# A graph layer's table stage: issue order of SyncE, load order, first columns, one helper's engine and one layout

## The chip, the cores and the metric

The kernel runs on one core of one Trainium2 chip. The metric is device time in microseconds for one launch. The engines are TensorE (PE; its weight loads are PEld), VectorE (DVE), ScalarE (ACT), GpSimd (POOL) and SyncE (SP), which here only issues DMAs and waits. Each engine works through its own queue in order.

## The reference

One relational graph layer on 625 nodes of width 512, with 20,625 edges sorted by destination, four relations, and a feed-forward block. Cut to what matters:

```python
h = max(layernorm(x), 0)
xs = h[src]
total_msg = sum over r of (xs @ W_rel[r] + b_rel[r]) * where(edge_type == r, edge_weight, 0)
agg = segment_sum(total_msg, dst) / max(segment_sum(edge_weight, dst), 1)
x1  = layer_norm(h + h @ W_self + b_self + agg)          # gain and bias ln1
ffn = gelu(x1 @ W_ffn1 + b_ffn1) @ W_ffn2 + b_ffn2
out = x + layer_norm(x1 + ffn)                           # gain and bias ln2
```

## The kernel before

Nodes stand in five blocks of 128 rows, edges in 162 tiles of 128. There are two stages.

**The table stage** computes h @ W_rel[r] for all nodes and the four relations: 20 steps (`table_rows(r, i)`, r outermost, step = 5r + i). A step is four matmuls, a scaled copy into `m` on ScalarE (L362, scaled by the inverse root that GpSimd computes, L310) and a DMA of `m` into a table in DRAM, issued by SyncE (L364). In the first five steps the next block of x is transposed in the middle of a step; VectorE computes its statistics (L343) and norm (L333) ahead of that. Two buffers hold relation weights, so the weights of relations 2 and 3 (L203) can load only when those of 0 and 1 are used up.

Messages are summed in two ways. For the **outer blocks** (0 and 4), whose edges are 31 and 32 tiles, the kernel builds a matrix of edge weights, destination by table row, and multiplies it with the kept `m`. The matrix lies in DRAM (`cells`): it is filled with zeros by a DMA (L227), then one weight per edge is scattered into it by an indirect DMA that GpSimd issues, one per column of 128 edges (L518, followed by a tiny fill, L521; 63 in all), and at last it is read back by SyncE (`load_sums`, L529), which must wait for that block's scatters. VectorE prepares columns in pieces (`line_sums`, L504 to L512: equal edges near each other are found by comparing keys and their weights added, 8 columns at a time). The place of each edge's cell comes from `line_columns`: five operations on VectorE, then twelve small ones (L468 to L480) on GpSimd.

For the **inner blocks** the message rows are gathered: in **the edge stage** GpSimd issues 99 indirect DMAs that fetch 128 rows each from the table (L942), and six for first edges (L1004). ScalarE and VectorE scale and add the rows of neighbouring tiles (L951, L969), TensorE sums them by destination with one-hot matrices (L980, L997), and the norms, the feed-forward block and the stores follow block by block. Eight buffers hold gathered rows.

Also in the table stage, the **degrees** are computed: the edge weights are split in three bfloat16 parts and written by relation into `w3` (L558), one-hot matrices `oc` are made by comparison (L581), and 172 small matmuls sum them (L599); a column of ones counts the edges. From the counts, `first_edges` finds each node's first edge group, and three indirect DMAs fetch these (L621).

What sets the order: VectorE, ScalarE, TensorE and GpSimd run in the order in which the code of the table stage is written (`manual_schedule`); SyncE's order there is left to the scheduler of the framework. Constants say at which step something is written: `COLUMNS_AT` (pieces), `LINE_AT` (the second block's places), `LOAD_AT` (the first `load_sums`), `PACE` (three scatters per step), and so on. In the edge stage a planner (`Plan`) lays out the order of all engines from estimated costs; `free = {"POOL": 3.0}` is when it lets GpSimd start, `LATE` when the second block's sums are there, both counted from the table's last matmul.

Of the kernel before, what the change touches and what calls it, by code (L numbers as in the profile page):

```python
# [16 lines left out]
P = 128  # L17
# [55 lines left out]
class Plan:  # L73
# [31 lines left out]
    def times(self):  # L105
        left, order, t = list(self.ops), [], 0.0
        free, buffers, back = {"POOL": 3.0}, dict(self.buffers), []
# [33 lines left out]
def gnn_layer(ctx, tc, x, edges, edge_line, edge_groups, w_self, w_rel, w_ffn1, w_ffn2, rows_in, brel_in, bf1_in, out, n_edges):  # L141
# [96 lines left out]
    load_x(2, 3)  # L238
    clear_cells(OUTER[0])
    load_x(3, NB)  # L240
# [208 lines left out]
    def line_columns(b, n):  # L449
# [17 lines left out]
        e = nc.gpsimd  # L467
# [74 lines left out]
    def degree_columns():  # L542
# [12 lines left out]
        w3 = early.tile([P, NT, DW], BF16, name="w3")  # L555
        nc.vector.memset(w3[:, :, DW - 1:DW], 1.0)
        for r in range(R):
            nc.vector.scalar_tensor_tensor(  # L558
                w3[:, :, r:DW - 1:R].rearrange("p t k -> p k t"), typ_f.unsqueeze(1).to_broadcast([P, 3, NT]), float(r), part,
                op0=ALU.is_equal, op1=ALU.mult)  # L560
# [26 lines left out]
    def degree_sums(j0, nj, oc, w3):  # L587

        for j in range(j0, j0 + nj):
            s = ep.starts[j]  # L590
            lo, hi = max(s, 0), min(s + W, NP)
            for q in range(lo // D, (hi - 1) // D + 1):
# [6 lines left out]
                nc.tensor.matmul(pdeg[q][:DW, a - q * D:z_ - q * D], w3[:, j, :], oc[:, j - j0, a - s:z_ - s],  # L599
# [215 lines left out]
    COLUMNS_AT, LINE_AT = (0, 2, 4, 7, 10, 12, 13, 14), 5  # L815
    LOAD_AT = (2, 4)
# [6 lines left out]
    LATE = 12.0  # L823
# [3 lines left out]
    DEGREES_AT, SPREAD_AT, FIRST_AT = (2, 3), (2, 4), (3, 0)  # L827
    chunks = [(j0, min(DG, NT - j0)) for j0 in range(0, NT, DG)]
    pieces = [(b, k, min(k + PIECE, n)) for b, _, n in outer for k in range(0, n, PIECE)]
    with tc.manual_schedule(engines={PE, DVE, ACT, mybir.EngineType.Pool}):  # L830
# [6 lines left out]

        def next_norm(i):
            nonlocal stats
            if i < NB:  # L840
                pre_norm(i, stats)
            if i + 1 < NB:
                stats = x_stats(i + 1)
# [9 lines left out]
        next_norm(0)  # L853
        hots, made = [], 0
        for k, n in ((0, 1), (1, 1), (2, 2)):
            transposed(hT[0][:, k:k + n, :], z[:, 0, k * P:(k + n) * P], f"h0_{k}")
        pre_norm(1, stats)
        line_columns(OUTER[0], sizes[OUTER[0]])
        stats = x_stats(2)
        for r in range(R):  # L860
            for i in range(NB):
                def next_transposed():
                    transposed(hT[i + 1], z[:, i + 1, :], f"h{i + 1}")
                    next_norm(i + 2)

                table_rows(r, i, next_transposed if r == 0 and i + 1 < NB else None)
                step = r * NB + i
                if step in COLUMNS_AT:
                    next_columns()
                if step == LINE_AT:  # L870
                    line_columns(OUTER[1], sizes[OUTER[1]])
                    set_limits(0)
                    for b in OUTER:
                        line_check(b, sizes[b])
# [422 lines left out]
```

## Time and profile before

| | |
|---|---|
| median of three runs | 303.07 us (301.33 to 303.23) |
| the profiled execution | 301.95 us |
| its span, first to last instruction | 300.1 us |
| PE / DVE / ACT / POOL busy | 249.5 / 186.3 / 67.6 / 199.0 us |
| mean granted TensorE clock | 0.934 |

Lines of the profile begin with a start and a duration in microseconds where they come from a view in order of time; a bracket at the end gives how long the engine stood before it, and what ended that. Groups give busy time, mean nanoseconds of one, then the standing time before them. "SPq" is SyncE's queue: an entry's duration there is the time of issuing. A row of stretches gives the stretch and its length, then pairs of busy time and count for the engines asked for, then granted clock, the share of the DMA engines and GB/s.

### The profile page before, as it was taken

How to read it: one execution, taken by the hardware profiler on the slowest of the kernel's cores; microseconds unless marked ns; L12 is line 12 of the kernel's file. 1: busy time of each engine (PE TensorE's matmuls, PEld its weight loads, DVE VectorE, ACT ScalarE, POOL GpSimd, SP SyncE). 2: the span in 40 equal slices, each digit the busy share in tenths (PEclk: the TensorE clock that was granted, in tenths of full speed). 3: DMA queues.
4: the chain of work that ended last, by engine and by line, in shares of the span. 5: the costliest groups of instructions: out<-in, count | busy, mean ns of one | idle time of the engine just before them, and what ended most of it. 6: DMA issues, size and time to landing. Idle time of an engine off the chain costs nothing.

```text
span 300.1 us, 3286 instructions
## 1 busy us (share of the span) xinstructions
PE 249.5 (83%) x1031; PEld 135.0 (45%) x1031; DVE 186.3 (62%) x417; ACT 67.6 (23%) x126; POOL 199.0 (66%) x287
## 2 busy tenths in 40 slices
PE   6869999995008999207999999899999999999891
PEld 2424444472003543003444444447659486673870
DVE  2599899999400700040468855697968889884714
ACT  2212111200000120004322221234314045250330
POOL 3638898888888888427777777677777777741000
PEclk9998999999555999956999999999999999999998
DMA  7997974000099300646667666666666776761101
GB/s 204 383 382 285 340 262 172 0 3 0 11 324 399 108 0 0 166 164 206 210 209 214 207 207 200 184 206 210 208 195 205 240 216 206 234 187 31 38 2 37
DMA packets 23743, 52.93 MB, mean 176 GB/s; under 512 B 4717, under 2 KB 8813, under 8 KB 23338
## 3 DMA queue, kind: packets, MB, share of 16 engines
q0 software_dynamic: 10512, 27.59, 31.2%
q1 hardware_dynamic: 13064, 24.97, 23.8%
q8 instruction: 9, 0.15, 0.2%
q10 hardware_dynamic: 146, 0.13, 0.1%
q14 instruction: 12, 0.10, 0.1%
HBM read 43.50 MB, written 9.18 MB: 176 GB/s over the span
## 4 chain that ended last, share of the span: by engine, by line
DMA 34%; POOL 33%; issue 15%; DVE 10%; PE 5%; ACT 1%; SPq 1%; POOLq 0%; DVEq 0%; ACTq 0%
POOL cells L518 23%; DMA ms<-table,row_i 22%; DMA xs<-in_x_dram 4%; POOL ms L942 4%; DMA ms_first<-table,x_row 4%; PE pu L736 2%; DMA table<-m 2%; PE po L754 2%; DVE ea L969 2%; POOL idle L521 2%; DVE z L1009 1%; DVE z L1000 1%; DMA cells<-weight,cell 1%; ACT ea L951 1%; POOL ms_first L1004 1%
## 5 line engine op out<-in xcount | busy, mean ns | idle before, releaser
L942 POOL DMA_INDIRECT ms<-table,row_i x99 | 95.6, 966 | 39.7 <-issue 23.0
L358 PE MATMUL pt<-wr,hT 128*128 128x512 f32 x160 | 74.9, 625 | 21.2 <-DMA wr<-in_L_gnn_W_rel_dram 21.2
L518 POOL DMA_INDIRECT cells<-weight,cell x63 | 71.5, 1134 | 18.1 <-issue 13.0
L358 PEld LDWEIGHTS pt<-wr,hT 128*128 128x128 f32 x160 | 31.2, 200 | 59.2 <-issue 58.9
L997 PE MATMUL acc<-es,oh 128*128 128x512 f32 x58 | 30.7, 628 | 15.2 <-ACT es L951 15.2
L969 DVE SCALAR_TENSOR_TENSOR ea<-ms,wgt_g,ea 128x512 f32<-128x512 f32 x40 | 30.0, 751 | 17.7 <-DMA ms<-table,row_i 14.0
L736 PEld LDWEIGHTS pu<-x1T,w_sb 128*128 128x128 f32 x320 | 37.6, 192 | 6.4 <-issue 3.8
L736 PE MATMUL pu<-x1T,w_sb 128*128 128x128 f32 (+1 forms) x320 | 38.3, 276 | 1.8 <-ACT gT L740 1.1
L951 ACT ACTIVATE ea<-ms,ed 128x512 f32<-128x512 f32 x30 | 20.7, 692 | 75.7 <-DMA ms<-table,row_i 54.7
L1075 PE MATMUL acc<-m,sums_w 128*128 128x512 f32 x80 | 36.4, 596 | 0.0
L754 PE MATMUL po<-w_sb,gT 128*128 128x512 f32 (+3 forms) x96 | 36.2, 522 | 0.0
L362 ACT ACTIVATE m<-pt,rx 128x512 f32<-128x512 f32 x20 | 13.7, 687 | 79.1 <-PE pt L358 79.1
L1075 PEld LDWEIGHTS acc<-m,sums_w 128*128 128x128 f32 x80 | 15.2, 193 | 19.7 <-issue 19.7
L754 PEld LDWEIGHTS po<-w_sb,gT 128*128 128x128 f32 (+1 forms) x96 | 16.6, 189 | 15.6 <-issue 13.5
L997 PEld LDWEIGHTS acc<-es,oh 128*128 128x128 f32 x58 | 11.1, 198 | 25.4 <-ACT es L951 17.3
L1009 DVE SCALAR_TENSOR_TENSOR z<-acc,rdeg,z 64x512 f32<-64x512 f32 (+1 forms) x13 | 9.7, 746 | 15.3 <-PE acc L997 15.1
L374 PE MATMUL pz<-ws_sb,hT 128*128 128x512 f32 x40 | 17.9, 594 | 0.8 <-DVE n_out L422 0.8
L969 DVE SCALAR_TENSOR_TENSOR es<-ms,wgt_g,ea 128x512 f32<-128x512 f32 x20 | 14.8, 742 | 2.3 <-DMA ms<-table,row_i 2.0
L740 ACT ACTIVATE gT<-pu,bf 128x128 f32<-128x128 f32 (+1 forms) x40 | 13.4, 361 | 10.9 <-PE pu L736 10.9
L951 ACT ACTIVATE es<-ms,ed 128x512 f32<-128x512 f32 x9 | 6.5, 721 | 28.8 <-DMA ms<-table,row_i 28.8
L614 DVE TENSOR_SCALAR xw<-first_edges 128x3 f32<-128x3 f32 x1 | 0.2, 163 | 20.0 <-PE first_edges L611 20.0
L374 PEld LDWEIGHTS pz<-ws_sb,hT 128*128 128x128 f32 x40 | 7.5, 190 | 9.9 <-issue 9.9
(174 smaller groups left out, 246.6 us busy)
## 6 DMA issues: line engine op xcount, KB each, us to landing
table<-m SPq DMA_DIRECT2D x20, 256.0 KB, 7.1
w_sb<-in_L_gnn_W_ffn_dram SPq DMA_DIRECT2D x2, 2048.0 KB, 11.0
wr<-in_L_gnn_W_rel_dram SPq DMA_DIRECT2D x3, 1024.0 KB, 9.8
cells<-zeros SPq DMA_DIRECT2D x2, 1280.0 KB
sums_w<-cells SPq DMA_DIRECT2D x2, 1280.0 KB
ms<-table,row_i POOLq DMA_INDIRECT x99, 3.6
rows<-in_rows_dram SPq DMA_DIRECT2D x1, 1536.0 KB, 10.3
ws_sb<-in_L_gnn_W_self_dram SPq DMA_DIRECT2D x1, 1024.0 KB, 6.0
```

The costliest lines, as they stand in the source:

```text
L358: nc.tensor.matmul(p, hT[i][:, k, :], wr_sb[r][:, k, :], start=(k == 0), stop=(k == KD - 1))
L362: nc.scalar.activation(m, p, AF.Copy, scale=rx[:, i, 1:2])
L374: nc.tensor.matmul(p[0], hT[i][:, k, :], ws_sb[:, k, :], start=(k == 0), stop=(k == KD - 1))
L518: i = nc.gpsimd.indirect_dma_start(out=cells[b][:, :], out_offset=bass.IndirectOffsetOnAxis(ap=cell[b][:, k:k + 1], axis=0), in_=weight[b] ...
L736: nc.tensor.matmul(pu[:, :nn], w1_sb[:, k, f * P:(f + 1) * P], x1T_b()[:, k, :nn], start=(k == 0), stop=(k == KD - 1))
L740: nc.scalar.activation(box["gT"][:, f, :nn], pus[f][:, :nn], AF.Gelu, bias=bf1[:, f:f + 1])
L754: nc.tensor.matmul(po[h][:n, :w], box["gT"][:, f, at], w2_sb[:, f, c], start=(f == 0), stop=(f == KF - 1))
L942: nc.gpsimd.indirect_dma_start(out=ms[j], out_offset=None, in_=table[:, :], in_offset=bass.IndirectOffsetOnAxis(ap=row_i[:, j:j + 1], axis=0))
L951: nc.scalar.activation(box["sum"], ms[j], AF.Copy, scale=wgt[:, j:j + 1])
L969: nc.vector.scalar_tensor_tensor(to, ms[j], wgt_g[:, k, q - 1:q], box["sum"], op0=ALU.mult, op1=ALU.add)
L997: nc.tensor.matmul(acc[bs], ohs[0][:, q, :].bitcast(F32), box["sum"], start=start, stop=last)
L1075: nc.tensor.matmul(acc[b,], sums_w[b][:, c, :], kept[c], start=False, stop=last)
```

## The change

- SyncE joins the engines that run the table stage in written order, so its DMAs go out in the order in which the code names them: each step's store, `later_loads(r)` after each relation, `load_sums` of block 0 at step 16, that of block 4 after all steps.
- Block 3 of x is loaded ahead of the first zero fill; block 4 behind it.
- The first piece of columns has four columns and not eight; nine pieces at other steps. The statistics of a block are written later, behind the pieces.
- `line_columns` takes its engine as an argument: the second block's twelve place operations run on VectorE. The ten fills of `lim` go to the start.
- `w3` is laid out [P, DW, NT] and not [P, NT, DW]: L558 writes it by column, and the degree matmuls read their 13 weights with a step of NT.
- Steps for edge columns, degree columns, one-hot comparisons, degree sums and first edges are set anew; scatters that are left over are all written at step 17. Checks move later. The planner lets GpSimd start at 15 and the second sums come at 17.

```diff
-        free, buffers, back = {"POOL": 3.0}, dict(self.buffers), []
+        free, buffers, back = {"POOL": 15.0}, dict(self.buffers), []
...
     load_x(2, 3)
+    load_x(3, 4)
     clear_cells(OUTER[0])
-    load_x(3, NB)
+    load_x(4, NB)
...
-    def line_columns(b, n):
+    def line_columns(b, n, e):
...
-        e = nc.gpsimd
...
-        w3 = early.tile([P, NT, DW], BF16, name="w3")
-        nc.vector.memset(w3[:, :, DW - 1:DW], 1.0)
+        w3 = early.tile([P, DW, NT], BF16, name="w3")
+        nc.vector.memset(w3[:, DW - 1, :], 1.0)
...
-                w3[:, :, r:DW - 1:R].rearrange("p t k -> p k t"), typ_f.unsqueeze(1).to_broadcast([P, 3, NT]), float(r), part,
+                w3[:, r:DW - 1:R, :], typ_f.unsqueeze(1).to_broadcast([P, 3, NT]), float(r), part,
...
-                nc.tensor.matmul(pdeg[q][:DW, a - q * D:z_ - q * D], w3[:, j, :], oc[:, j - j0, a - s:z_ - s],
+                nc.tensor.matmul(pdeg[q][:DW, a - q * D:z_ - q * D], w3[:, :, j], oc[:, j - j0, a - s:z_ - s],
...
-    COLUMNS_AT, LINE_AT = (0, 2, 4, 7, 10, 12, 13, 14), 5
-    LOAD_AT = (2, 4)
+    FIRST_PIECE = 4
+    COLUMNS_AT, LINE_AT = (0, 1, 3, 5, 6, 8, 10, 12, 14), 7
+    EDGES_AT, COLUMNS_OF_EDGES_AT, HOTS_AT = 4, 9, (9, 11, 11, 13, 13, 14)
+    LOAD_AT = 16
...
-    LATE = 12.0
+    LATE = 17.0
...
-    DEGREES_AT, SPREAD_AT, FIRST_AT = (2, 3), (2, 4), (3, 0)
+    DEGREES_AT, SPREAD_AT, FIRST_AT = 15, 16, 17
...
-    with tc.manual_schedule(engines={PE, DVE, ACT, mybir.EngineType.Pool}):
+    with tc.manual_schedule(engines={PE, DVE, ACT, mybir.EngineType.Pool, mybir.EngineType.SP}):
...
+        set_limits(0)
+        set_limits(1)
         pre_norm(1, stats)
-        line_columns(OUTER[0], sizes[OUTER[0]])
+        line_columns(OUTER[0], sizes[OUTER[0]], nc.gpsimd)
         stats = x_stats(2)
...
                 if step in COLUMNS_AT:
                     next_columns()
+                if step + 3 < NB:
+                    stats = x_stats(step + 3)
                 if step == LINE_AT:
-                    line_columns(OUTER[1], sizes[OUTER[1]])
-                    set_limits(0)
-                    for b in OUTER:
-                        line_check(b, sizes[b])
-                while columns and (sent < PACE * (step + 1) or step >= NB):
+                    line_columns(OUTER[1], sizes[OUTER[1]], nc.vector)
+                while columns and sent < PACE * (step + 1):
                     scatter(*columns.pop(0))
                     sent += 1
...
+                if step == FIRST_AT:
+                    while columns:
+                        scatter(*columns.pop(0))
                     first_edges()
                     load_first_edges()
```

More of the change, by code (lines that the diff above doesn't have):

```diff
@@ L826, in gnn_layer @@
     PARTED = 1, 2
-    DEGREES_AT, SPREAD_AT, FIRST_AT = (2, 3), (2, 4), (3, 0)
+    DEGREES_AT, SPREAD_AT, FIRST_AT = 15, 16, 17
     chunks = [(j0, min(DG, NT - j0)) for j0 in range(0, NT, DG)]
-    pieces = [(b, k, min(k + PIECE, n)) for b, _, n in outer for k in range(0, n, PIECE)]
-    with tc.manual_schedule(engines={PE, DVE, ACT, mybir.EngineType.Pool}):
+    pieces = [(OUTER[0], 0, FIRST_PIECE)]
+    for b, _, n in outer:
+        pieces += [(b, k, min(k + PIECE, n)) for k in range(FIRST_PIECE if b == OUTER[0] else 0, n, PIECE)]
+    with tc.manual_schedule(engines={PE, DVE, ACT, mybir.EngineType.Pool, mybir.EngineType.SP}):
         nc.scalar.activation(gelu_of, ones, AF.Gelu)
@@ L852, in gnn_layer @@
             nc.tensor.matmul(warm, zeros[:, :P], zeros, start=True, stop=True)
-        next_norm(0)
-        hots, made = [], 0
+        pre_norm(0, stats)
+        stats = x_stats(1)
+        hots = []
         for k, n in ((0, 1), (1, 1), (2, 2)):
             transposed(hT[0][:, k:k + n, :], z[:, 0, k * P:(k + n) * P], f"h0_{k}")
+        set_limits(0)
+        set_limits(1)
         pre_norm(1, stats)
-        line_columns(OUTER[0], sizes[OUTER[0]])
+        line_columns(OUTER[0], sizes[OUTER[0]], nc.gpsimd)
         stats = x_stats(2)
@@ L889, in gnn_layer @@
                     nc.vector.tensor_add(xs[:, i, :], xs[:, i, :], b2_bc)
-                if (r, i) == (3, 0):
-                    for g_bc in (g1_bc, g2_bc):
-                        nc.vector.tensor_scalar(g_bc, g_bc, 1.0 / RS, None, op0=ALU.mult)
-                if (r, i) > (1, 1) and made < len(chunks):
-                    hots.append(degree_hots(*chunks[made], *cols))
-                    made += 1
-                if (r, i) == DEGREES_AT:
+                if step == DEGREES_AT:
+                    group_columns()
                     for made_ in hots:
@@ L899, in gnn_layer @@
                     spread_rows = degree_end()
-                if (r, i) == SPREAD_AT:
+                if step == SPREAD_AT:
                     spread_rows()
-                if (r, i) == FIRST_AT:
+                    for b in OUTER:
+                        line_check(b, sizes[b])
+                if step == FIRST_AT:
+                    while columns:
+                        scatter(*columns.pop(0))
                     first_edges()
                     load_first_edges()
-                if (r, i) == (2, NB - 1):
+                if step == R * NB - 2:
                     total_outside = count_outside()
+                    for g_bc in (g1_bc, g2_bc):
+                        nc.vector.tensor_scalar(g_bc, g_bc, 1.0 / RS, None, op0=ALU.mult)
             later_loads(r)
```

21 lines of the change are left out of this document (8 added, 13 removed).

## The prediction

> **What bounds the kernel now.** I read the page's engine table and costliest groups first, then GpSimd in order of time, then SyncE's queue, because the chain that ended last names GpSimd and its DMAs most.
>
> ```profile
> span 300.1 us, 3286 instructions
> PE 249.5 (83%) x1031; PEld 135.0 (45%) x1031; DVE 186.3 (62%) x417; ACT 67.6 (23%) x126; POOL 199.0 (66%) x287
> L942 POOL DMA_INDIRECT ms<-table,row_i x99 | 95.6, 966 | 39.7 <-issue 23.0
> L518 POOL DMA_INDIRECT cells<-weight,cell x63 | 71.5, 1134 | 18.1 <-issue 13.0
> ```
>
> TensorE is busier in total, but two trains of indirect DMAs on GpSimd fill most of the span: 63 scatters of the outer blocks' edge weights (L518), then 99 gathers of table rows (L942) and six at L1004. GpSimd in order of time, with the table store from the chain that ended last:
>
> ```profile
> 20.29 1.26 POOL L518 DMA_INDIRECT cells<-weight,cell  x1 [5.07 <-DVE weight L512]
> 119.24 0.96 POOL L518 DMA_INDIRECT cells<-weight,cell  x1 [0.22 <-issue]
> 120.50 1.00 POOL L621 DMA_INDIRECT x_edges<-in_edge_groups_dram,x_group  x1 [0.23 <-issue]
> 123.07 0.95 POOL L621 DMA_INDIRECT x_edges<-in_edge_groups_dram,x_group  x1 [0.30 <-issue]
> 124.57 7.30 DMA table<-m
> 132.97 0.99 POOL L942 DMA_INDIRECT ms<-table,row_i  x1 [8.94 <-issue]
> 265.93 0.95 POOL L942 DMA_INDIRECT ms<-table,row_i  x1 [0.30 <-DVE el L959]
> ```
>
> So the span has three parts: up to the first gather 132.97; the 105 gathers 132.97 to 266.88, that is 133.9 (1.275 each); a tail of 33.2 behind the last gather. Just ahead of the first gather GpSimd stands 8.94, of which 0.30 is the usual gap: it waits for the last table stores, which land at 124.57 + 7.30 = 131.87. Why these are late, SyncE's queue shows (in order of time, then its waits), with the matmul that stood still for it:
>
> ```profile
> 42.86 3.75 SPq L364 DMA_DIRECT2D table<-m  x2
> 81.08 0.32 SPq L529 DMA_DIRECT2D sums_w<-cells  x1
> 81.98 0.38 SPq L203 DMA_DIRECT2D wr<-in_L_gnn_W_rel_dram  x1
> 122.17 0.32 SPq L529 DMA_DIRECT2D sums_w<-cells  x1
> 122.59 2.31 SPq L364 DMA_DIRECT2D table<-m  x4
> SPq L529 <- DMA cells<-weight,cell: 57.5, 4, 33.0
> 91.32 6.19 PE L358 MATMUL pt<-wr,hT 128*128 128x512 f32 x8 [19.70 <-DMA wr<-in_L_gnn_W_rel_dram]
> ```
>
> SyncE waits twice at the head of its queue for scatters (L529). Behind the first stands the last relation's weight load (81.98), so TensorE waits 19.70; behind the second stand the last four table stores, issued only at 122.59. Two chains therefore end close together at 124 to 133: GpSimd's own queue (free at 123.07 + 0.95 + 0.30 = 124.3) and the table (131.9). A change must shorten both.
>
> **Part 1: SyncE in written order.** The last four stores no longer stand behind the second L529, nor the weights behind the first. TensorE's table chain, from ScalarE's rows:
>
> ```profile
> 31.91 0.69 ACT L362 ACTIVATE m<-pt,rx 128x512 f32<-128x512 f32 x1 [2.75 <-PE pt L358]
> 62.65 3.49 PEld L599 LDWEIGHTS <-w 128*13 128x13 bf16 x128
> wr<-in_L_gnn_W_rel_dram SPq DMA_DIRECT2D x3, 1024.0 KB, 9.8
> ```
>
> The row at 31.91 is step 4 of 20; a step is 0.69 + 2.75 = 3.44. Step 4 comes no later (x blocks 3 and 4 load separately, the third ahead of the zero fill), so 15 steps end at 31.9 + 15 x 3.44 = 83.5; the degree sums add 172 x 27 ns (3.49 / 128) = 4.7 and the small first-edge matmuls about 1: 89. A store takes 7.3 to land: the table is there at 97 with its copy. Each moved issue: the second zero fill, weights 2, rows and the self weights now follow the store of step 4 (33 instead of from 13.11 on); weights 2 land by about 43 to 46, wanted at 31.9 + 5 x 3.44 = 49. Weights 3 follow step 9's store, 49 + 9.8 = 59, wanted at 66. The fill is wanted by scatter 32, at about 65. The first L529 sits behind the store of step 16 (78); its 31 scatters are done at about 64 (16.2 + 31 x 1.265, two roots, and the disturbance of part 4), so the three stores behind it lose nothing. The second L529 comes last; only output stores are queued behind it. Its issue follows the last scatter by 1.7 (122.17 against 120.5) and its sums land 4 to 10 later, so 2 to 8 after the first gather; the planner's new figures (17 against 15) put them 2 after. TensorE has the first outer block's twenty products to do meanwhile. Cost taken as nothing; if that cover fails, 3 to 5.
>
> One new dependence on VectorE: the degree sums at step 15 want all six comparisons (L581 below), written out at steps 9 to 14. VectorE ends the last at about 69 (75 by part 4, less some 6 of work behind it); TensorE arrives at 31.9 + 11 x 3.44 = 70. Level; what VectorE is late, the table is late.
>
> Alone, this part gains at most 132.97 - 124.3 = 8.7: then GpSimd's queue is late next.
>
> **Part 2: scatters start sooner.** Around the first scatter:
>
> ```profile
> 14.44 0.25 POOL L480 TENSOR_TENSOR place<-place,line_s 128x31 f32<-128x31 f32 x1
> 15.19 0.69 DVE L343 BATCH_NORM_STATS2 st_x<-xs 128x6 f32<-128x512 f32 x1 [3.01 <-DMA xs<-in_x_dram]
> 19.30 0.69 DVE L512 TENSOR_REDUCE weight<-same 128x8 f32<-128x512 f32 x1
> ...
> L558 DVE SCALAR_TENSOR_TENSOR w<-fl,part 128x486 bf16<-128x486 f32 x4 | 8.9, 2517 | 0.3 <-DVE part L554 0.3
> L504 DVE TENSOR_TENSOR same<-key 128x1016 f32<-128x1016 f32 x7 | 8.4, 1206 | 0.0
> L581 DVE TENSOR_TENSOR oc<-rel,row_w 128x1026 bf16<-128x1026 bf16 x6 | 7.2, 1235 | 0.0
> L512 DVE TENSOR_REDUCE weight<-same 128x8 f32<-128x512 f32 x7 | 4.8, 687 | 0.2
> L511 DVE TENSOR_TENSOR same<-same,line 128x512 f32<-128x512 f32 x7 | 4.8, 685 | 0.0
> L445 DVE SCALAR_TENSOR_TENSOR row_i<-fl 128x162 int32<-128x162 f32 x1 | 0.3, 319 | 0.0
> ```
>
> Today VectorE stands 3.01 for x blocks 3 and 4 before it makes the first eight columns. In the changed order the statistics of block 3 come behind the first piece. VectorE stands from 15.19 - 3.01 = 12.2 on; there it makes the comparison of four columns (half of 1206), waits for the places (14.44 + 0.25), and then needs three small operations, half of 685 and half of 687: done about 15.9, first scatter 16.2 instead of 20.29. **-4.1**. The fifth scatter needs the second piece: 15.9, then statistics of a block and eight columns (15.19 to 19.99 today, 4.8), and a norm of 0.7: 21.4. GpSimd, with four scatters and the root of block 3 between them, gets there at about 22, so no wait is added; later the pace of three per step asks 3 x 1.265 = 3.8 of GpSimd in a step of 3.44, so TensorE's steps never hold it. Bounds: 15.5 (the places themselves) to 19 (block 3 no earlier).
>
> **Part 3: the second block's places off GpSimd.** Scatters stop here (in order of time; then GpSimd's busy time in that stretch; then the scatters' alone by stretch):
>
> ```profile
> 47.11 0.09 POOL L521 MEMSET idle<- 1x1 f32 x1
> 55.96 1.07 POOL L518 DMA_INDIRECT cells<-weight,cell  x1 [0.15 <-issue]
> ...
> 47.12:55.90 8.78, 7.90 (x24) 1.00 0.17 63
> ...
> 20.20:36.40 16.20, 12.15 (x10) 0.89 0.88 318
> 36.40:46.10 9.70, 8.43 (x4) 1.00 0.85 286
> 55.90:72.90 17.00, 13.80 (x11) 1.00 0.02 1
> 72.90:78.60 5.70, 4.42 (x4) 0.76 0.02 0
> 78.60:120.40 41.80, 31.70 (x33) 0.79 0.44 151
> ```
>
> Without the twelve place operations and ten fills the scatter at 55.96 would start at 47.42: **-8.5**. The fills go ahead of the first places, where GpSimd has nothing else. On VectorE the twelve cost 0.2 to 0.32 each (the last is L445's for 162 elements; these have 32), 2.4 to 3.8, paid for in part 4. Checks, group columns and the scaling of rows move later on VectorE, which stands for 20 today while the weights are late; they cost nothing unless VectorE is late at step 17, and then the table's 13 of slack (below) cover it.
>
> **Part 4: degree weights by column, and what remains beside VectorE.** An undisturbed scatter is 31.70 / 33 = 0.96, and 1.265 from start to start. While L558 runs, four take 8.43, 4.6 too much. In the other three stretches with VectorE busy, 25 take 30.37, 6.4 too much in 38.9: 0.165 per us. L558 writes elements 26 bytes apart; contiguous, 486 elements are three times the 162 of L445, bounded below by L504's rate (1206 x 486 / 1016 = 0.58) and above by three whole L445, 0.96; I take 0.66, near the lower end, because L445's fixed part is paid once. VectorE saves 8.9 - 4 x 0.66 = 6.3 and the lump of 4.6 becomes ordinary disturbance. VectorE is then busy until about 75 (today 78; 3.0 of standing and 6.3 less, 3 for the places, some 3 of waits on TensorE), so the new disturbance is 0.165 x (75 - 16.2) = 9.7, where it was 4.6 + 6.4 = 11.0. **-1.3**. Bounds: 6 (the lump gone, nothing added) to 14 (the new operations disturb like L558 does).
>
> The degree matmuls now read 13 weights 324 bytes apart instead of 26 bytes in a row. No row shows such a read; it can cost nothing, or a little, or what rival 3 works out. I take zero, since the table (97) is hidden behind GpSimd's queue (110 in the sum) for 13: 13 / 172 = 76 ns on each. [...]
>
> **The sum.** The next instruction behind the scatters starts at 120.5 - 4.1 - 8.5 - 1.3 = 106.6. Three x_edges gathers take 3.8 (120.50 to 124.3): first gather at 110.4, while the table is there at 97. Gain 132.97 - 110.4 = 22.6. The 105 gathers and the tail keep their 167.1. TensorE is nearly full there (the first pair is its busy time, by stretch):
>
> ```profile
> 155.00:267.00 112.00, 110.12 (x469) 65.62 (x468) 88.55 (x187) 34.62 (x71) 84.45 (x88) 1.00 0.70 210
> ```
>
> 110.12 of 112 is 98%. From 89 to 110 it can do products that need no gather, more of them than now, since the planner lets GpSimd start at 15 rather than 3; that relieves it. But queues in another order can lose as well, so zero, with 4 either way. Span 300.1 - 22.6 = 277.5. The profiled execution took 301.95, 1.85 over its span: 279.3; the median of the runs, 303.07, is 1.1 above the profiled one. I say **279.5**.
>
> **Rivals.**
> 1. *The edge stage gives some back.* Gathers now start before the second sums have landed and while first_columns waits for x_edges. If an in-order queue puts such a wait ahead of the consumers, the ring of eight gather buffers (8 x 1.25 = 10) runs full and GpSimd stops. For it: TensorE's 98%. Against: today's planner has the first gather 3 behind the table products, whose last stores are issued 10.4 before it (122.59 to 132.97); wrong by 7 or more, the stage still lost only 133.9 - 105 x 1.25 = 2.6 (1.25 = the 0.95 of a gather and the gap of 0.30). Price 4 to 10: 284 to 290.
> 2. *The edge stage gains.* TensorE enters it with more work done, the 2.6 vanishes, and the last sums stop waiting behind other products: 273 to 275.
> 3. *The strided weights make TensorE the bound.* If the loads stop overlapping, each costs what one degree matmul lasts in the row below, 179 instead of 27 ns: 172 x 0.152 = 26, table at 123, gain 10: 292. **Slower** it becomes from (22.6 + 13) / 172 = 0.21 us more on each. If every one of the 13 columns took as long as the whole load does now, 13 x 27 = 0.35, TensorE would lose 172 x 0.32 = 56, the table come at 153, and the kernel take 322. Against it: that would be a tenfold price on a load that today hides within the 27 ns of its matmul.
>
> ```profile
> L599 PE MATMUL pdeg<-oc,w x172: 164/179/181, 62.9 to 67.4; 128*13 128x38 bf16 x145, 128*13 128x33 bf16 x4, 128*13 128x21 bf16 x3, 128*13 128x25 bf16 x3
> ```
>
> 4. *The change does half of what it says:* the table comes early but the scatters stay as they are (VectorE, made fuller, disturbs them as much as it relieves them): gain 8.7 plus part of the 12.6 of parts 2 and 3, say 15: 287.
>
> **Chances.** The forecast (276 to 283.5) 0.70; rival 1 0.10; rival 2 0.08; rival 3 short of slower 0.04, slower 0.03; rival 4 0.04; no difference from a cause that I don't see 0.01. The range 273 to 288 leaves out part of rivals 1 and 3 and the last. A difference of 1%, 3 us, is about what a measurement of this kernel can tell: faster 0.95, same 0.02, slower 0.03.
>
> **What would show it.** The first L942 near 110 with GpSimd coming straight from L621 (gap 0.30, no wait for the table). First L518 near 16, no POOL operation of the places between scatters, and L518's total near 70. Both L529 with no table store behind a wait. The four w3 operations at about 0.66. TensorE without a stop for wr, the last m near 89. First to last gather near 134, tail near 33. A first gather that waits for table<-m again would make me wrong, and then the degree matmuls' spacing is the first thing to read.

## The result and the profile after

The changed kernel takes **294.81 us** (median of 4 runs, 293.98 to 295.51) where the kernel before, on the same chip, takes 303.15: 0.974 of it, 95% interval 0.969 to 0.979. The forecast was 279.5 with a range of 273 to 288. The sign is right, and the gain is about a third of what was forecast. The profiled execution took 295.31, with a span of 293.4. (On some chips, in some hours, the kernel before took 345 to 348, about 14% more, and the changed kernel 340, about 15% more; the runs that fell there stand in a table of their own, and their times are compared among themselves only.)

The stretch up to the first gather came out somewhat better than forecast. GpSimd in the changed kernel, in order of time, and SyncE's queue below it:

```profile
15.21 1.28 POOL L518 DMA_INDIRECT cells<-weight,cell  x1 [0.99 <-DVE weight L512]
...
102.55 0.96 POOL L518 DMA_INDIRECT cells<-weight,cell  x1 [0.22 <-issue]
103.81 1.01 POOL L621 DMA_INDIRECT x_edges<-in_edge_groups_dram,x_group  x1 [0.23 <-issue]
...
107.64 0.95 POOL L944 DMA_INDIRECT ms<-table,row_i  x1 [0.30 <-issue]
...
131.76 0.94 POOL L944 DMA_INDIRECT ms<-table,row_i  x1 [1.74 <-DVE ea L971]
...
138.66 0.95 POOL L944 DMA_INDIRECT ms<-table,row_i  x1 [4.69 <-ACT ea L953]
...
151.94 0.95 POOL L944 DMA_INDIRECT ms<-table,row_i  x1 [6.94 <-DVE ea L971]
...
255.14 0.95 POOL L944 DMA_INDIRECT ms<-table,row_i  x1 [0.30 <-issue]
```

```profile
75.11 0.32 SPq L529 DMA_DIRECT2D sums_w<-cells  x1
78.52 8.08 SPq L365 DMA_DIRECT2D table<-m  x3
105.34 0.32 SPq L529 DMA_DIRECT2D sums_w<-cells  x1
```

No store stands behind the second wait any more, and the first gather starts at 107.64 (132.97 before), straight from L621 with a gap of 0.30. That is 25.3 earlier. But the last gather ends at 256.09 and the span at 293.4, so 14.5 are lost again among the gathers and 4.1 behind them. The rows of the two stretches, gathers and tail, kernel before first (stretch and length, then busy time and count of TensorE, its weight loads, VectorE, ScalarE and GpSimd, then granted clock, DMA share, GB/s):

```profile
132.97:266.88 133.91, 127.87 (x504) 73.22 (x505) 95.03 (x195) 42.86 (x83) 101.30 (x105) 0.97 0.69 207
266.88:300.10 33.22, 25.54 (x131) 17.37 (x129) 15.33 (x43) 6.43 (x15) 1.00 (x2) 0.97 0.12 38
```

```profile
107.64:256.09 148.45, 134.66 (x510) 76.55 (x511) 99.98 (x215) 43.36 (x83) 104.30 (x105) 0.92 0.64 195
256.09:293.40 37.31, 24.26 (x115) 18.18 (x113) 13.90 (x38) 6.62 (x14) 0.58 (x2) 0.81 0.08 27
```

In the list above, GpSimd's three stops (1.74, 4.69, 6.94) end with VectorE or ScalarE work on gathered rows: the ring of eight buffers is full, because the rows are not used. Beyond the usual 0.30 the three make 12.5 of the 14.5. Why the rows are not used, TensorE and then VectorE of the changed kernel show:

```profile
85.37 13.90 PE L375 MATMUL pz<-ws_sb,hT 128*128 128x512 f32 x32
114.42 5.88 PE L375 MATMUL pz<-ws_sb,hT 128*128 128x512 f32 x8 [15.16 <-DVE z L379]
...
121.28 3.70 PE L1077 MATMUL acc<-m,sums_w 128*128 128x512 f32 x8
124.82 1.88 PE L999 MATMUL acc<-es,oh 128*128 128x512 f32 x4
```

```profile
111.32 0.18 DVE L627 CAST x_cols<-x_edges 128x27 f32<-128x27 int32 x1 [25.06 <-DMA x_edges<-in_edge_groups_dram,x_group]
...
113.63 2.72 DVE L379 SCALAR_TENSOR_TENSOR z<-pz,rx,z 128x512 f32<-128x512 f32 x4
```

TensorE's queue now begins with all five self parts (h @ W_self, L375). Four PSUM buffers serve them, so the fifth waits for VectorE's first add (L379). That add stands in VectorE's queue behind `first_columns` (L627), which waits 25.06 for the first-edge gathers. So TensorE stands 15.16, then does the fifth self part and four products, and the first sum of gathered rows (L999) starts at 124.82: 17.2 behind the first gather. Before it was 4.2 (137.13 against 132.97). TensorE stood 15.16 there too, but with nothing left to do between the stand and that sum:

```profile
137.13 3.78 PE L997 MATMUL acc<-es,oh 128*128 128x512 f32 x4 [15.16 <-ACT es L951]
```

### The profile page after: what moved, and what is told of

It reads as the page before. It is cut to its first block, busy times and chain, and to the rows that moved or that the text cites. A ratio compares the mean times of both kernels' runs of the same rounds, so it can differ in the third digit from the quotient of the medians.

```text
span 293.4 us, 3291 instructions
## 1 busy us (share of the span) xinstructions
PE 255.0 (87%) x1031; PEld 140.3 (48%) x1031; DVE 183.8 (63%) x436; ACT 68.4 (23%) x126; POOL 191.8 (65%) x275
## 4 chain that ended last, share of the span: by engine, by line
PE 34%; DVE 26%; DMA 15%; POOL 15%; issue 7%; ACT 1%; SPq 0%; POOLq 0%; DVEq 0%; ACTq 0%
PE acc L1077 12%; POOL cells L518 11%; DMA ms<-table,row_i 9%; PE pu L736 7%; PE acc L999 5%; PE po L754 5%; DVE same L504 3%; DMA ms_first<-table,x_row 3%; PE pz L375 2%; DVE oc L581 2%; DVE earlier L506 2%; DVE ea L971 2%; DVE weight L512 2%; DMA x_edges<-in_edge_groups_dram,x_group 2%; DVE same L511 1%
## 5 line engine op out<-in xcount | busy, mean ns | idle before, releaser
L944 POOL DMA_INDIRECT ms<-table,row_i x99 | 98.6, 996 | 42.6 <-issue 15.2
L518 POOL DMA_INDIRECT cells<-weight,cell x63 | 68.4, 1085 | 13.9 <-issue 12.5
L359 PE MATMUL pt<-wr,hT 128*128 128x512 f32 x160 | 70.9, 597 | 1.4 <-DMA wr<-in_L_gnn_W_rel_dram 1.4
L359 PEld LDWEIGHTS pt<-wr,hT 128*128 128x128 f32 x160 | 29.9, 192 | 36.4 <-issue 36.3
L736 PEld LDWEIGHTS pu<-x1T,w_sb 128*128 128x128 f32 x320 | 42.1, 212 | 6.6 <-issue 3.1
L736 PE MATMUL pu<-x1T,w_sb 128*128 128x128 f32 (+1 forms) x320 | 42.6, 297 | 1.6 <-ACT x1T L1099 1.3
L1077 PE MATMUL acc<-m,sums_w 128*128 128x512 f32 x80 | 38.0, 619 | 0.0
L754 PE MATMUL po<-w_sb,gT 128*128 128x512 f32 (+3 forms) x96 | 36.0, 522 | 0.0
L375 PE MATMUL pz<-ws_sb,hT 128*128 128x512 f32 x40 | 19.8, 654 | 15.2 <-DVE z L379 15.2
L999 PE MATMUL acc<-es,oh 128*128 128x512 f32 x58 | 29.6, 609 | 0.7 <-DVE es L971 0.7
L754 PEld LDWEIGHTS po<-w_sb,gT 128*128 128x128 f32 (+1 forms) x96 | 16.8, 189 | 17.1 <-issue 14.8
L375 PEld LDWEIGHTS pz<-ws_sb,hT 128*128 128x128 f32 x40 | 8.3, 211 | 26.4 <-DVE z L379 16.0
L627 DVE CAST x_cols<-x_edges 128x27 f32<-128x27 int32 x1 | 0.2, 180 | 25.1 <-DMA x_edges<-in_edge_groups_dram,x_group 25.1
L764 DVE TENSOR_TENSOR y<-po,z 128x512 f32<-128x512 f32 (+3 forms) x6 | 3.6, 599 | 19.3 <-PE po L754 19.2
L999 PEld LDWEIGHTS acc<-es,oh 128*128 128x128 f32 x58 | 10.7, 195 | 9.0 <-issue 6.2
```

The source lines that it names most:

```text
L359: nc.tensor.matmul(p, hT[i][:, k, :], wr_sb[r][:, k, :], start=(k == 0), stop=(k == KD - 1))
L375: nc.tensor.matmul(p[0], hT[i][:, k, :], ws_sb[:, k, :], start=(k == 0), stop=(k == KD - 1))
L518: i = nc.gpsimd.indirect_dma_start(out=cells[b][:, :], out_offset=bass.IndirectOffsetOnAxis(ap=cell[b][:, k:k + 1], axis=0), in_=weight[b] ...
L736: nc.tensor.matmul(pu[:, :nn], w1_sb[:, k, f * P:(f + 1) * P], x1T_b()[:, k, :nn], start=(k == 0), stop=(k == KD - 1))
L754: nc.tensor.matmul(po[h][:n, :w], box["gT"][:, f, at], w2_sb[:, f, c], start=(f == 0), stop=(f == KF - 1))
L944: nc.gpsimd.indirect_dma_start(out=ms[j], out_offset=None, in_=table[:, :], in_offset=bass.IndirectOffsetOnAxis(ap=row_i[:, j:j + 1], axis=0))
```

## The experiments

**Which of the planner's figures?** The order of the edge stage comes from the planner, to which the change gives two new figures, POOL (when GpSimd may start) and LATE (when the second block's sums are there). Theory A blamed the figures together and then LATE: the planner has one load engine, takes the operation with the longest tail first, and with 17 puts the second block's load ahead of the first block's, so that five self parts go ahead of the twenty products. Rival B blamed POOL. The first run gives both old figures back:

```diff
-        free, buffers, back = {"POOL": 15.0}, dict(self.buffers), []
+        free, buffers, back = {"POOL": 3.0}, dict(self.buffers), []
...
-    LATE = 17.0
+    LATE = 12.0
```

> The planner's two figures put back (3 and 12), once more, in the hope of a run in which TensorE's short matmuls keep their 27 ns. Where the kernel before takes 303: theory A 276 to 280, theory B 290 to 296. Where it takes 345: 329 to 337 as before, and nothing new.

Measured: **279.83** (278.94 to 280.51) against 304.25 for the kernel before, 0.921 (0.915 to 0.926). Its two stretches, gathers and tail, and TensorE's first sum of gathered rows:

```profile
109.31:244.76 135.45, 128.34 (x503) 72.98 (x504) 97.44 (x208) 42.55 (x82) 101.75 (x105) 0.97 0.73 211
244.76:278.50 33.74, 25.92 (x133) 17.68 (x132) 15.65 (x45) 6.85 (x16) 1.01 (x2) 0.96 0.12 38
```

```profile
114.22 3.75 PE L999 MATMUL acc<-es,oh 128*128 128x512 f32 x4 [17.19 <-issue]
```

Nearly all of the loss is gone: the first gather is at 109.31, the first sum 4.9 behind it, and the stretches take 135.5 and 33.7 where the forecast kept 133.9 and 33.2. TensorE's operations come in the order of the kernel before again, but for 16 table matmuls. So the two figures together cost what the forecast missed. Next, POOL alone (LATE stays 17):

```diff
-        free, buffers, back = {"POOL": 15.0}, dict(self.buffers), []
+        free, buffers, back = {"POOL": 3.0}, dict(self.buffers), []
```

> Changed kernel with POOL 3 for 15 alone (LATE 17 stays), on another chip. Theory A (LATE's order of the loads is the cause): all five self parts still go ahead of the products, 290 to 297 where the kernel before takes 303, gathers 144 to 150. Rival B (POOL's figure is the cause): 279 to 284, gathers 134 to 138. On the chip where the kernel before took 347 this kernel took 0.971 of it against 0.952 and 0.963 with both old figures and 0.984 for the changed kernel, which lies between.

Measured: **276.04** (275.58 to 279.59) against 303.60, 0.911 (0.907 to 0.915): the lowest median of all (its interval touches that of the run before), and 0.936 of the changed kernel by the ratios to the kernel before (0.9109 / 0.9736). Its two stretches, and TensorE in order of time:

```profile
109.00:244.89 135.89, 129.94 (x507) 73.80 (x508) 97.66 (x211) 43.18 (x83) 103.58 (x105) 0.95 0.72 210
244.89:277.80 32.91, 25.30 (x128) 17.05 (x126) 15.13 (x41) 6.66 (x16) 1.01 (x1) 0.98 0.13 42
```

```profile
86.69 10.46 PE L375 MATMUL pz<-ws_sb,hT 128*128 128x512 f32 x24
114.05 6.22 PE L999 MATMUL acc<-es,oh 128*128 128x512 f32 x8 [16.89 <-issue]
...
128.11 3.70 PE L1077 MATMUL acc<-m,sums_w 128*128 128x512 f32 x8
```

Theory A had the order right and the cost wrong. The self parts still go first, and the products come later (128) than in the changed kernel (121). TensorE even stands 16.9. Rival B's cause holds, though its 279 to 284 is missed on the fast side. What differs is that only three self parts stand ahead of the first sums of rows, so these start at 114.05, 5.1 behind the first gather.

**The stop, or the plan?** Theory D says that the one stop of 15.16 is the loss; rival B, that POOL 15 orders the whole stage badly. This run keeps both new figures and tells the planner when x_edges are there, which puts VectorE's five adds ahead of `first_columns`:

```diff
-    first_ready = op("DVE", 2.4, first_columns, rank=(0.3,), level=1.5)
+    edges_there = op("EDGES", 18.5, None)
+    first_ready = op("DVE", 2.4, first_columns, after=[edges_there], rank=(0.3,), level=1.5)
```

> Changed kernel with POOL 15 and LATE 17 kept; the planner is told only that x_edges are there 18.5 after its start, so that VectorE's five adds of the self parts stand ahead of first_columns instead of behind it. Theory D (the loss is one stop: the fifth self part waits 15.2 for a PSUM buffer whose add stands behind first_columns, which waits for the x_edges gathers; the order of self parts and products costs nothing by itself): TensorE does the five self parts and the first four products without a stop from 85.4 to about 109, the first sum of edges starts at 113 to 115 as with POOL 3, GpSimd is stopped for under 3 in all, gathers 134 to 138, the whole 276 to 283. Rival B (POOL 15 spreads the orders of the whole edge stage wrongly): gathers stay at 143 or more and the whole at 288 to 296. If the kernel before takes 345 here, no verdict.

Measured: **286.62** (285.47 to 286.89) against 303.03, 0.947 (0.942 to 0.951): between the two, outside both expectations. Its stretches, and TensorE around the first sum and in the tail:

```profile
108.85:247.04 138.19, 126.04 (x495) 73.23 (x496) 96.93 (x211) 43.77 (x84) 102.93 (x105) 0.95 0.72 209
247.04:283.30 36.26, 22.91 (x113) 17.39 (x111) 13.53 (x36) 5.94 (x13) 0.57 (x1) 0.80 0.09 29
```

```profile
86.58 17.33 PE L375 MATMUL pz<-ws_sb,hT 128*128 128x512 f32 x40
...
113.87 3.75 PE L1000 MATMUL acc<-es,oh 128*128 128x512 f32 x4 [5.27 <-issue]
...
257.76 1.12 PE L318 MATMUL tp_x<-ident,x 128*128 128x128 f32 x4 [5.93 <-DVE x L701]
259.55 10.07 PE L736 MATMUL pu<-x1T,w_sb 128*128 128x128 f32 x64 [0.67 <-ACT x1T L1100]
```

The stop is gone, the first sum starts 5.0 behind the first gather with all five self parts done, and the gathers take 138.2 where they took 148.5. The traces of this run and of the changed kernel have the same operations in the same order on TensorE, ScalarE and GpSimd, and on VectorE but for these five adds. So nothing else is in it: the stop is worth about 10 among the gathers, and 8 in the median.

The rest comes with POOL 15, and the medians put it at 10.6 (286.62 against 276.04). The two profiled executions differ by 5.5 only, since that of POOL 3 is the slowest of its five: 2.3 among the gathers and 3.4 in the tail. The tail's part can be followed. TensorE stands 5.93 for the norm of the last block (L701), because all other feed-forward products are already done; with POOL 3 eight of their matmuls (L754) are kept for that time, and it stands 0.43:

```profile
251.58 3.60 PE L754 MATMUL po<-w_sb,gT 128*128 128x512 f32 x8
255.60 0.66 PE L318 MATMUL tp_x<-ident,x 128*128 128x128 f32 x4 [0.43 <-DVE x L701]
256.94 7.41 PE L736 MATMUL pu<-x1T,w_sb 128*128 128x128 f32 x64 [0.68 <-ACT x1T L1099]
```

The stand itself cost nothing: in both runs the transposes (L318) start 10.7 behind the end of the last gather (247.04 to 257.76, 244.89 to 255.60). What cost was the work behind it, which ran at a lower clock for some microseconds (the mean of this tail is 0.80, of that with POOL 3 0.98; last section): 10.07 and 1.12 where it takes 7.41 and 0.66, that is 3.1 of the 3.4.

**What the parts are worth up to the first gather.** Both runs start from the version with both old figures (279.83, first gather at 109.31). Part 1 taken out, SyncE ordered by the scheduler (in the edge stage's own list of engines too):

```diff
-    with tc.manual_schedule(engines={PE, DVE, ACT, mybir.EngineType.Pool, mybir.EngineType.SP}):
+    with tc.manual_schedule(engines={PE, DVE, ACT, mybir.EngineType.Pool}):
```

> The same kernel as i1 (POOL 3, LATE 12, SyncE ordered by the scheduler's own estimate), since the kernel before took 347 us there. In that trace six table stores stand behind the second wait for scatters and are issued from 107.9 on. If part 1 is what brings the table early: first gather at 115 to 118, waiting 5 to 9 for the table, the whole 285 to 290. If the scatters' end alone decides: first gather at 109, 278 to 282.

Measured: **287.25** (286.59 to 287.71), 7.4 more. SyncE and GpSimd:

```profile
105.07 0.32 SPq L529 DMA_DIRECT2D sums_w<-cells  x1
105.49 3.67 SPq L365 DMA_DIRECT2D table<-m  x6
```

```profile
116.70 0.95 POOL L944 DMA_INDIRECT ms<-table,row_i  x1 [9.17 <-issue]
```

Six stores stand behind the second wait, and GpSimd stands 9.17 for the table: the first gather comes 7.4 later, and the whole too. (GpSimd's own queue was ready 8.9 earlier, at 107.8; in this execution it had begun its scatters 1.5 sooner than in the run compared with, 15.38 against 16.86.) Part 3 taken out, the second block's places on GpSimd:

```diff
-                    line_columns(OUTER[1], sizes[OUTER[1]], nc.vector)
+                    line_columns(OUTER[1], sizes[OUTER[1]], nc.gpsimd)
```

> Changed kernel with POOL 3 and LATE 12 (279.8 as measured), and the second block's places made on GpSimd again, at the same step. By the prediction's part 3 (8.5 for twelve operations and ten fills between the scatters; the fills stay ahead of the first places here, so a little less): the last scatter ends 6 to 8.5 later (111 to 113), the first gather comes at 115 to 118, behind GpSimd's own queue with a gap of 0.3, the whole is 286 to 289. If the places hide in gaps between scatters that VectorE's disturbance makes anyway: under 2, 279 to 282.

Measured: **284.56** (284.54 to 285.58), 4.7 more. The first and the last of the twelve operations, the last scatter and the first gather:

```profile
46.36 0.36 POOL L468 TENSOR_SCALAR found<-line_f 128x32 f32<-128x32 f32 x1
...
50.09 0.25 POOL L480 TENSOR_TENSOR place<-place,line_s 128x32 f32<-128x32 f32 x1
...
107.98 0.96 POOL L518 DMA_INDIRECT cells<-weight,cell  x1 [0.21 <-issue]
...
113.07 0.95 POOL L944 DMA_INDIRECT ms<-table,row_i  x1 [0.30 <-issue]
```

The places stand between scatters from 46.36 to 50.34, 4.0; the first gather comes 3.8 later, behind GpSimd's own queue, though this execution too began its scatters 1.5 sooner: from the first scatter to the end of the last one it takes 93.6 for 88.3, 5.2 more. Neither expectation fits: the price is below the 6 to 8.5 and above the 2.

The kernel before paid more for the same twelve operations. There four of them ran beside VectorE's comparisons (L581, 50.34 to 53.93, then L504) and took 1.1 to 1.3 each; here VectorE stands meanwhile (14.6 before L508 and L509, which use what the twelve make, for 2.1 in the run compared with), and the same four take 0.22 to 0.25. One of the four, before and in this run:

```profile
51.73 1.11 POOL L477 TENSOR_TENSOR place<-place,line_f 128x32 f32<-128x32 f32 x1
...
49.15 0.24 POOL L477 TENSOR_TENSOR place<-place,line_f 128x32 f32<-128x32 f32 x1
```

**The runs at 345 to 348.** Thirteen runs fell where the kernel before took 345 to 348. They say nothing of the 303-us case by their times, but in all of them the table is late (its last `m` at 128 to 130) and the first gather comes at 131 to 133, so they compare orders of the edge stage alone. The first seven came before all runs told above, so theories stand in their expectations as they stood then. By edit:

Both old figures (edit as above), twice:

> The changed kernel with the planner's two figures put back (GpSimd from 3, second sums at 12), everything of the table stage as changed. Theory A (the loss lies in the planner's order: at 17 the planner's one load engine takes the second block's sums first, so TensorE gets all five self parts ahead of the first block's products and stands 15.2 at the fifth): the first gather stays near 107.6, the 105 gathers take 134 to 137 again and the tail 33, so 276 to 280. Theory B (the earlier start itself costs: gathers beside the load of the second sums, and a wait for x_edges right behind the start, in whatever order): 290 to 296, as the changed kernel.

> The planner's two figures put back (3 and 12), as in e1. Theory A (planner's order): ratio 0.91 to 0.92 (276 to 280 where before takes 303), first gather near 107.6, no stop of GpSimd over 2. Theory B (the earlier start costs in any order): 0.96 to 0.98.

The changed kernel itself, on such a chip:

> The changed kernel once more, unchanged, beside the two below, since the first four ran on a chip on which the kernel before took 348 and short matmuls came 0.5 to 2.6 us apart without a wait that the profile shows. Both theories: ratio to the kernel before 0.97 where the kernel before takes 303.

LATE alone, three times, and POOL alone:

```diff
-    LATE = 17.0
+    LATE = 15.0
```

> The changed kernel with one figure other: second sums at 15, not 17; GpSimd still from 15. In the planner this alone puts the first block's loads back in front, so the twenty products come ahead of the self parts. Theory A: TensorE does about 20 us of products from 86 on, no stop of 15, first edge sum 4 to 6 behind the first gather, 272 to 280. Theory B: 290 to 296.

> Changed kernel, one figure of the planner changed: LATE 15 for 17 (the second block's sums), POOL stays 15. Theory A (with LATE 17 the second block's load has a longer tail in the planner than the first block's load of length zero, the one modelled load engine takes it first, and so five self parts go ahead of the twenty products of the first block): at 15 the order of the loads turns back, the products go first again, so the gathers take about 134 to 136 and the whole is 279 to 283, against 294.8 for the changed kernel and 279.8 for it with both old figures. Rival B (the figure 15 for GpSimd's first gather is what spreads the orders wrongly): LATE alone moves little, 290 to 296, gathers 145 or more.

> The same kernel as the run before of this name (LATE 15, POOL 15), on another chip, since on that one the kernel before took 347 us, 13% over its own time. Theory A: 279 to 283 where the kernel before takes 303. Rival B: 290 to 296. With the kernel before near 347 again: 0.98 to 0.99 of it, and no verdict between the two.

> Changed kernel, the other figure alone: POOL 3 for 15, LATE stays 17. Theory A: all five self parts still stand ahead of the products, the fifth waits for VectorE's add behind first_columns until about 114, so the whole stays at 290 to 297 with gathers of 144 to 150 and GpSimd stopped for the consumers. Rival B: 280 to 284.

The plan with measured figures, three times:

```diff
-        free, buffers, back = {"POOL": 15.0}, dict(self.buffers), []
+        free, buffers, back = {"POOL": 22.0}, dict(self.buffers), []
...
-    LATE = 17.0
+    LATE = 26.0
...
-    first_ready = op("DVE", 2.4, first_columns, rank=(0.3,), level=1.5)
+    edges_there = op("EDGES", 25.5, None)
+    first_ready = op("DVE", 2.4, first_columns, after=[edges_there], rank=(0.3,), level=1.5)
...
-        m[b] = op("LOAD", 0.0 if b == OUTER[0] else LATE, None)
+        m[b] = op(f"LOAD{b}", 0.0 if b == OUTER[0] else LATE, None)
```

> The changed kernel with the planner told what its trace shows, counted from the last table product at 85.4: GpSimd from 22, second sums at 26 on a load engine of their own, x_edges at 25.5 (until now it had them at 0). Theory A: the first block's products and both outer self parts fill TensorE's wait, no in-order queue stands for x_edges; 270 to 277, at or below e2_late_15. Theory B: 290 to 296.

> The planner told the measured times (GpSimd 22, second sums 26 on a load engine of their own, x_edges 25.5), as in e3. Theory A: 270 to 277 where before takes 303, no stop of TensorE over 8 between its last table product and the first edge sum. Theory B: 290 to 296.

> Changed kernel with the planner told what its trace shows: first gather 22 behind its start, second sums at 26, the two loads on engines of their own, x_edges there at 25.5 so that first_columns stands behind that. If wrong figures in the planner are the whole matter (theory A widened), the twenty products fill TensorE from 89 on without a stop of 17 and the edge stage gains 2 to 4 on the two old figures: 275 to 279. Rival C (the gathers' own pace of 1.25 bounds the stage once the products are not late, and an order that starts the sums of edges late costs as much as it gains): 279 to 288.

SyncE by the scheduler, with the new figures (the table stage alone) and with the old ones (as above):

> The changed kernel with SyncE's order in the table stage left to the scheduler again; all else as changed. If part 1 of the prediction holds, a wait for scatters stands ahead of weights or table stores again: the table ends behind the scatters, first gather at 113 to 118 and not 107.6, so 5 to 11 slower than the changed kernel (300 to 306). If the written order of SyncE is worth nothing because GpSimd's queue is the last to be free anyway, the time stays within 2 of the changed kernel.

> Changed kernel with both old figures of the planner (279.8 as measured), and SyncE taken out of the written order again, in the table stage and in the edge stage, so that its queue is ordered by the scheduler's own estimate. If part 1 of the change is what brings the table early, the last stores stand again behind the scatters' waits, the first gather comes 8 to 15 later (117 to 124, table bound) and the whole is 288 to 295. If the scatters' end at 104 alone decides, it stays at 279 to 282.

> Changed kernel with POOL 3 and LATE 12 (279.8 as measured), and SyncE taken out of the written order, so that its queue is again ordered by the scheduler's own estimate. If part 1 is what brings the table early, the last stores stand again behind the wait for the last scatters (issued at about 107, landing at 114 to 116), the first gather comes 6 to 8 later (115 to 117, behind table stores) and the whole is 285 to 289. If the order that the scheduler finds for the new sequence already has the stores ahead of the waits, the first gather stays at 109 and the whole at 278 to 282.

| edit | first sum of rows starts | gathers take | time, as a share of the kernel before's on the same chip |
|---|---|---|---|
| both old figures (4 runs, two of them with SyncE by the scheduler) | 137.1 to 137.8 | 161 to 164 (three of them) | 0.952 to 0.970 |
| POOL 3 alone | 138.4 | 164 | 0.971 |
| LATE 15 alone (3 runs) | 149.0 to 150.1 | 168 to 170 | 0.988 to 0.993 |
| the changed kernel | 150.7 | 167 | 0.984 |
| the same with SyncE by the scheduler | 149.4 | 171 (its slowest execution) | 0.970 |
| plan with measured figures (3 runs) | 156.9 to 157.4 | 172 (two of them) | 1.004 to 1.011 |

The table falls into three groups by the start of the first sum of gathered rows (137 to 138, 149 to 151, 157), whether products or self parts go first. One row of the middle group lies at the time of the first: the changed kernel with SyncE by the scheduler, whose times lie far apart (336.4 to 344.2) and decide nothing. With LATE 15 and in the plan with measured figures all twenty products stand ahead of that sum, and the second of these is the slowest. The forecast's "relief" (more products early) costs here about 5% against the old figures (medians of 348 to 350 against 333 to 335). Whether LATE 15 and the measured plan cost as much in the 303-us case was not seen.

## Why the prediction was wrong, point by point

**Up to the first gather: right, and nearly term by term.** Scatters start at 15.21 (forecast 16.2, bounds 15.5 to 19), the last m's step ends near 86 (89), the three x_edges gathers begin at 103.81 (106.6), the first gather at 107.64 (110.4) with the table long there. Of the 25.3 gained, 5.1 are the earlier start of the scatters (4.1 forecast), 11.6 their shorter train (99.9 to 88.3; forecast 8.5 and 1.3), and 8.6 the wait for the table that is gone (8.7). Some 1 to 2 us of this are the luck of one execution: in three runs with the same table stage (both old figures, POOL 3, x_edges told to the planner) the scatters start at 16.4 to 16.9 and the first gather at 108.9 to 109.3. The groups behind the terms, the degree matmuls in order of time, and their weight loads in the kernel before and in the changed one (shortest, median and longest in nanoseconds):

```profile
L518 POOL DMA_INDIRECT cells<-weight,cell x63 | 68.4, 1085 | 13.9 <-issue 12.5
L558 DVE SCALAR_TENSOR_TENSOR w<-fl,part 128x486 bf16<-128x486 f32 x4 | 2.3, 645 | 0.0
```

```profile
65.38 3.39 PE L599 MATMUL pdeg<-oc,w 128*13 128x21 bf16 x128
```

```profile
L599 PEld LDWEIGHTS <-w x172: 85/87/89, 62.6 to 67.4; 128*13 128x13 bf16 x172
L599 PEld LDWEIGHTS <-w x172: 98/100/102, 65.2 to 69.9; 128*13 128x13 bf16 x172
```

- *Part 1* was to gain at most 8.7 alone; taken out, it costs 7.4. That two chains end close together, and that a change must shorten both, holds: with SyncE back the table is late, with the places back GpSimd is.
- *Part 3* was sized right for the kernel before: of the 11.6 that the train of scatters lost, 3.1 are the scatters' own time (71.5 to 68.4) and 8.5 all the rest, places and fills. The fills are under 0.8 of that. Put back into the finished version, the places cost 3.8 to 5.2, with VectorE standing beside them where it ran comparisons before. So what a part saves and what it costs to take it out again were two figures here.
- *Part 4* was sized small: 3.1 for 1.3. The four w3 operations take 645 ns each (0.66 taken), and all scatters 68.4 (near 70).
- *Rival 3* is out: with the 13 weights read 324 bytes apart, 128 degree matmuls take 3.39, 26.5 ns each, as before. A load does take longer, 100 ns in the median for 87, but the loads overlap (172 of them, 17.2 us together, start between 65.2 and 69.9) and the matmuls keep their pace, so nothing of it reaches the time.

**The step that failed: "The 105 gathers and the tail keep their 167.1."** They took 185.8: 14.5 more among the gathers, 4.1 in the tail. The forecast put "queues in another order" at zero, with 4 either way, though the change hands the planner two new figures and so lets it order the whole edge stage anew. With the old figures the two stretches take 169.2, and the kernel 279.8. What the runs showed in place of the zero has two parts:

- *The stop*, 8.2 in the median, 10.3 among the gathers. The mechanism had been named in rival 1 almost word for word (a wait for x_edges ahead of the consumers, a full ring), and its price of 4 to 10 was right; its chance of 0.10 was too low. A late first sum isn't absorbed: in the changed kernel it came 13.0 later relative to the first gather (17.2 against 4.2), and GpSimd's stops came to 12.5.
- *The rest of the order under POOL 15*, 6.8 in the median against both old figures and 10.6 against POOL 3 alone. No rival named it.

Two sentences of the forecast were wrong with it:

- "TensorE has the first outer block's twenty products to do meanwhile." They were no cover; TensorE's queue held the self part that waits for VectorE first. A cover has to stand ahead of the wait in the same queue, and the trace before could not show the new order.
- "that relieves it" (products before 110). TensorE at 98% seemed to need relief. But the two fastest versions stand 16.9 and 17.2 ahead of the first sum.

**The tail's 4.1** was not in the forecast at all. In the changed kernel TensorE stands 5.93 ahead of the last transposes, as in the run with x_edges told to the planner, and the transposes and 64 matmuls behind it take 3.4 more than in the kernel before (11.47 against 8.07) at a lower clock (0.81 over the tail for 0.97; last section). So this is shown for most of the 4.1.

Rival 1 is thus part of what happened, at its price. Rival 2 is out, since the edge stage lost; rival 4 is out, since the scatters did get shorter. Not settled: which wait of the later plan makes up the 2 to 3 among the gathers that remain with POOL 15 once the stop is gone, and why the medians put POOL 15 at more than the traces do.

## What to carry to other kernels

Take the start of the first consumer, not the mean load of an engine, as the figure to watch where a ring of buffers feeds an in-order queue: list what stands ahead of that consumer in its queue, and for each entry what it waits for, through the other engines' queues too. A change of a planner's figures is a change of the whole order behind it, and is tried alone before it is shipped with edits that it was meant to follow. Keep some work of TensorE for a wait that can't be avoided: here the transposes started 10.7 behind the last gather with and without such work, but they and the 64 matmuls took 8.1 with it and 11.2 without. Where two chains end within a few microseconds, price each part by taking it out of the finished version, and expect another figure than it saved in the old one.

## What the hardware showed

**TensorE after standing.** Behind every stand of 4.2 us or more in the traces of the 303-us case (the shortest: 4.21, in the run with x_edges told to the planner) the work runs slower for some microseconds: in the kernel before and the changed one the granted clock was 0.50 at the end of each, and in the other runs four matmuls of 512 columns took 3.5 to 3.8 for 1.88 (with POOL 3 eight took 6.22 for 3.60), four transposes 1.12 for 0.66. In the changed kernel's tail, stretches behind the stop of 5.93 (columns as above), and the work behind two such stops:

```profile
268.00:272.00 4.00, 3.33 (x15) 2.92 (x16) 0.54 (x1) 0.76 (x2) 0.00 (x0) 0.50 0.17 66
272.00:276.00 4.00, 4.00 (x21) 4.00 (x21) 0.00 (x0) 0.93 (x3) 0.00 (x0) 0.52 0.02 4
276.00:280.00 4.00, 4.00 (x37) 4.00 (x37) 0.00 (x0) 1.47 (x4) 0.00 (x0) 1.00 0.00 0
```

```profile
237.31 1.11 PE L318 MATMUL tp_x<-ident,x 128*128 128x128 f32 x4 [4.49 <-DVE x L701]
...
267.87 1.11 PE L318 MATMUL tp_x<-ident,x 128*128 128x128 f32 x4 [5.93 <-DVE x L701]
269.65 10.36 PE L736 MATMUL pu<-x1T,w_sb 128*128 128x128 f32 x64 [0.67 <-ACT x1T L1099]
```

The clock is about 0.5 until 276, 8 us after work resumed at 267.87. Four transposes take 1.11 behind either stop and 0.66 behind a stand of 0.43; the 64 matmuls take 10.36 and 7.41. A stop in the tail therefore cost 3.1 to 3.4 more behind it, even where the wait itself was hidden. How long a stand has to be is not shown. Behind one of 0.43 the work is at full speed. Behind one of 2.96 in the kernel before (20.44) four transposes took 0.66, but then the clock fell to 0.50 (21.3 to 24.7), and eight table matmuls took 5.29 for 3.60. In the changed kernel it was 0.50 from 153.0 to 156.4 too, and there the longest stand in the 5 us ahead was 0.76. How long the clock stays low, these two kernels show. Where matmuls follow the stand without a gap it was 3.7 to 5.1 (137.13 to 140.8 and 91.32 to 96.4 in the kernel before, 114.42 to 118.8 in the changed one), and 7.8 and 8.0 behind the two stops of the changed kernel above (237.31 to 245.1, 267.87 to 275.9), where four transposes and a gap of 0.67 come first. That the gap is what lengthens it is not shown.

**The runs at 345 to 348.** In them the degree matmuls, 26.5 ns apart above, arrive singly with gaps in which TensorE waits for nothing that the profile shows. The changed kernel on such a chip:

```profile
L599 PE MATMUL pdeg<-oc,w 128*13 128x38 bf16 (+3 forms) x172 | 9.7, 194 | 36.3 <-issue 36.3
```

The gaps end at 108.6, 3 us after GpSimd's last scatter (105.65), while the scatters themselves keep their pace (16.8 to 105.65, 88.9 for 88.3). That the scatters are behind the gaps is not shown. The edge stage is slower there too (gathers of 161 to 164 against 135 with the old figures). Three chips were met in both conditions, so it doesn't belong to a chip. The cause is open.
